# Softmax denominators turned by DMA instead of TensorE, and the values' bias folded into the output bias

## The chip, the cores and the metric

The kernel runs on one core of one Trainium2 chip. The metric is the device time of one execution in microseconds (us). The engines of the core are named as in the profile: PE (TensorE, matmuls), DVE (VectorE), ACT (ScalarE), POOL (GpSimd) and SP (SyncE, which here only issues DMAs). PE writes its products to PSUM, everything else lies in SBUF.

## The reference

The input is x, 16 batches of 512 tokens with 512 features. A layer norm is followed by an attention block and a gated FFN that run side by side on the normed x; both are added to x.

```python
xn = layernorm(x)
q, k, v = split(xn @ w_qkv.T + b_qkv)            # 16 heads of 32
attn = softmax(mask(q @ k.T / sqrt(32)))         # causal, 512 x 512 per head
a = (attn @ v) @ w_out.T + b_out
g, u = (xn @ gate_w.T) * gate_s, (xn @ up_w.T) * up_s   # 1408 wide, weights -1, 0, 1
f = ((silu(g) * u) @ down_w.T) * down_s
out = x + a + f
```

Everything is float32 in the reference.

## The kernel before

**Halves.** A float32 operand is held as two float16 tiles, a high half h and a low half l = x - h. A product of two such operands is three matmuls (h h, h l, l h). The FFN weights are exact in 8 bits and need one tile, so a product there is two matmuls. A "full" matmul contracts 128 rows and streams 512 columns. Making the halves is the work of the other engines: usually ACT casts the high half and POOL or DVE subtracts.

**Slots.** Work is cut into 64 slots, one for each batch b and group g of four heads. In slot s PE computes the scores of group s (`soft_run`, three runs of query blocks: block 3, block 2, blocks 1 and 0) and the value product of group s - 1 (`av_step`); in between it works on fillers: the q and k projections of the next group (`qk_proj`), the values of a batch (`v_proj`, in its first slot), FFN chunks (`ffn_chunk`), the down projection (`down_tile`, in the last slot of a batch) and the output projection of the batch before (`out_tile`).

**The softmax.** DVE adds the mask and takes the row maximum (L559), ACT takes the exponential and sums each row (L564) into `den`, 16 columns of 128 query rows: four query blocks by four heads. ACT and DVE split the exponentials into the halves `pq` (L584, L589), and SP issues a DMA transpose of each query block's `pq` into `pT` (L598). `pT` has single buffers, `pq` two.

**The denominators.** The value product comes out with (head, feature) on the 128 partitions and the 512 queries along the row, so it has to be multiplied by a tile that holds 1/den of the query, the same on the 32 partitions of a head. `av_step` makes it so: DVE takes the reciprocal `rden` (L618), POOL spreads each of its 16 columns over 32 (`rb`, L621), PE transposes the four 128x128 blocks of `rb` against an identity into the PSUM tile `R` (L631), and ACT copies `R` to SBUF as `Rs` (L634). After the value product `av` (72 matmuls of 32 columns of the array, four side by side, L644), DVE multiplies it with `Rs` (L657), ACT casts the high half `oh` (L658) and POOL subtracts to `ol` (L659). `out_tile` takes these.

**The values.** `v_proj` has 12 full matmuls for each of four token blocks. DVE scales the PSUM tile and adds the bias `bv_b`, which a DMA has spread to all partitions (L497), ACT casts `vh` (L500), POOL subtracts `vl` (L503).

**PSUM.** Projections, FFN tiles and `R` share three buffers with the tag "mm"; scores have four ("s1"), the value product one ("av").

**What sets the order.** The order on every engine is written out by a planner, `Plan`. Each step has an engine, a duration that the source assumes, what it reads and writes, and for PE a key: its wanted place in time. `Plan.order` simulates the five engines and the buffers with these durations; PE takes the lowest key among the steps that could start, the others the step that has been ready longest (plus a slack that the source gives). The resulting lists are fixed; at run time each engine goes through its list in order, and semaphores make it wait for what it reads. `attention_slot` gives the value product its key by `AV_LAG`, 7 us after the start of its slot, and the transposes of `R` 1.5 us before it. SP's list mixes the transposes of `pq`, those of the normed x of the next batch (`xh`, `xl`, L414), loads and stores.

**The bound checks.** A second, general path follows when a count of checked ranges is short of 48; on these inputs it isn't run.

Of the kernel before, what the change touches and what calls it, by code (L numbers as in the profile page):

```python
# [14 lines left out]
ALU = mybir.AluOpType  # L15
# [14 lines left out]
def newton_rsqrt(nc, y, v, t):  # L30

    yi = y.bitcast(I32)
    nc.vector.tensor_scalar(yi, v.bitcast(I32), 1, None, ALU.logical_shift_right)
    nc.vector.tensor_scalar(yi, yi, -1, 0x5F3759DF, ALU.mult, ALU.add)
    for _ in range(3):
        nc.vector.scalar_tensor_tensor(t, v, -0.5, y, ALU.mult, ALU.mult)
        nc.vector.tensor_tensor(t, t, y, ALU.mult)
        nc.vector.scalar_tensor_tensor(y, t, 1.5, y, ALU.add, ALU.mult)

# [23 lines left out]
class Plan:  # L63
# [34 lines left out]
    def order(self):  # L98
# [6 lines left out]
        made, done, dma = {}, [], 0.0  # L105

# [22 lines left out]
        while len(done) < len(self.steps):  # L129
            best = None  # L130
            for e in self.ENGINES:
                cands = [(max(t, free[e]), st) for t, st in ((begin(st), st) for st in ready[e]) if t is not None]
                if not cands:
                    continue
# [29 lines left out]
def fast_path(ctx, tc, good, x, wqkvT, bqk, bv, woT, bo, wgT, wuT, wdT, gs, us, dsc, out):  # L164
# [19 lines left out]
    def tmp32(name):  # L184
        return work(name, "tmp32", 4)
# [13 lines left out]
    bv_b = cp.tile([P, 512], F32, name="bv_b")  # L199
# [22 lines left out]
    grp = {}  # L222
# [20 lines left out]
    def mm_group(f, ps, ops, piece=4, first=0, n=None):  # L243
# [9 lines left out]
        prev = []  # L253
# [66 lines left out]
    def small_constants():  # L320
        gsus = work("gsus", "r32", 1)
        gs_c, us_c = (lambda: gsus()[:, 0:IC]), (lambda: gsus()[:, IC : 2 * IC])
        for dst, src, tok in ((bv_b, bv, "bv"), (ds_b, dsc, "ds"), (bo_b, bo, "bo")):
# [6 lines left out]
        add(  # L330
            "DVE", dve(512), lambda: nc.vector.tensor_scalar(bv_b, bv_b, 32.0, None, ALU.mult),
            r=["bv"], w=["bv"],
        )
        absmax(42, bqk_c[:, 0:4], ["bqk"])
        absmax(43, bqk_c[:, 4:8], ["bqk"])
        absmax(44, bv_b, ["bv"])
# [34 lines left out]
    def ln_stats(b, slack):  # L371
# [17 lines left out]
        add("DVE", 2.0, rstd, r=[(mv, tb) for tb in range(NT)], w=[v, y, t], slack=slack)  # L389
# [56 lines left out]
    def qk_proj(f, b, g, which):  # L446
# [15 lines left out]
            ],  # L462
        )
# [13 lines left out]
    def v_proj(f, b, tb):  # L477
        s = st[b]
        ps, t = mm(f"v_{b}_{tb}"), tmp32(f"vt_{b}_{tb}")
        if tb == 0:  # L480
# [12 lines left out]
            ],  # L493
        )
        add(
            "DVE", dve(512),
            lambda: nc.vector.scalar_tensor_tensor(t(), ps(), 2.0 ** -13, bv_b, ALU.mult, ALU.add),  # L497
            r=[ps, "bv"], w=[t], slack=-3,
        )
        add("ACT", act(512), lambda: nc.scalar.copy(vh()[:, tb, :], t()), r=[t], w=[(vh, tb)], slack=4)  # L500
        add(
            "POOL", gps(512),
            lambda: nc.gpsimd.tensor_tensor(vl()[:, tb, :], t(), vh()[:, tb, :], ALU.subtract),  # L503
            r=[t, (vh, tb)], w=[(vl, tb)], slack=2,
# [3 lines left out]
    def soft_run(b, g, blocks):  # L508
# [31 lines left out]
        def exps(i):  # L540
# [4 lines left out]
            "PE", 0.3 + 3 * cols / 2400.0, scores, r=[qh, ql, kh, kl],  # L545
# [31 lines left out]
        for i in blocks:  # L577
# [10 lines left out]
                "DVE", dve(4 * n),  # L588
# [12 lines left out]
            base += 8 * n  # L601
        return run

    def av_step(b, g):
# [6 lines left out]
        rb = work("rb_" + nm, "tmp32", 4)  # L611
        R = mm("R_" + nm)
        r = work("Rs_" + nm, "r32", 1)
# [4 lines left out]
        add("DVE", 0.15, lambda: nc.vector.reciprocal(rden(), d["den"]()), r=dens, w=[rden], slack=2)  # L618
        add(
            "POOL", gps(512),  # L620
            lambda: nc.gpsimd.tensor_scalar(  # L621
                rb().rearrange("p (c d) -> p c d", d=32),
                rden().unsqueeze(2).to_broadcast([P, 16, 32]),
                2.0 ** -15, None, ALU.mult,
            ),
            r=[rden], w=[rb],
        )

        def spread():
            for i in range(4):  # L630
                nc.tensor.transpose(R()[:, i * P : (i + 1) * P], rb()[:, i * P : (i + 1) * P], ident)  # L631

        first = add("PE", 0.5, spread, r=[rb], w=[R], lat=0.3)
        add("ACT", act(512), lambda: nc.scalar.copy(r(), R()), r=[R], w=[r], slack=-3)  # L634

        def run():
# [16 lines left out]
        second = add(  # L653
            "PE", 2.3, run, r=[("pT", i) for i in range(4)] + [(t, tb) for t in (vh, vl) for tb in range(NT)],
            w=[av], lat=0.3,
        )
        add("DVE", dve(512), lambda: nc.vector.tensor_tensor(r(), av(), r(), ALU.mult), r=[av, r], w=[r], slack=-2)  # L657
        add("ACT", act(512), lambda: nc.scalar.copy(oh(), r()), r=[r], w=[oh], slack=3)  # L658
        add("POOL", gps(512), lambda: nc.gpsimd.tensor_tensor(ol(), r(), oh(), ALU.subtract), r=[r, oh], w=[ol])  # L659
        return first, second  # L660
# [138 lines left out]
    def count_good(when, key):  # L799
        ps, ps1, limits = mm("flagT"), mm("flagR"), tmp32("limits")  # L800
# [8 lines left out]
        def set_limits():  # L809
# [9 lines left out]
            nc.gpsimd.memset(hi[:, 44:45], 64 * 32.0)  # L819
# [22 lines left out]
    def attention_slot(s):  # L842

        av, runs = (), []
# [7 lines left out]
        def place(t0, T):  # L852
            for k, step in enumerate(av):
                step.key = t0 + AV_LAG + (k - 1) * 1.5 if s < NSLOT else t0
            t = t0
            for step, c in runs:
                step.key = t
                t += T * c / sum(c for _, c in runs)

# [4 lines left out]
    AV_LAG = 7.0  # L864
    ends = []

    def fillers(s):
# [10 lines left out]
        if b > 0 and g in (1, 3):  # L878
            for tb in range(late) if g == 1 else range(late, NT):
                out_tile(f, b - 1, tb)  # L880
        for ic in range(CUTS[g], CUTS[g + 1]):
            ffn_chunk(f, b, ic)
        if g == 0 and b > 0:
# [42 lines left out]
    for s in range(NSLOT):  # L926
# [9 lines left out]
        if s == 2:  # L936
            for kc in range(KC):
                load_wo(kc)
        if g == 0 and b + 1 < NB:
            ln_load(b + 1, when)  # L940
            ln_stats(b + 1, 6.0)
            for tb in range(NT):
                ln_norm(b + 1, tb, 6.0)
                ln_turn(b + 1, tb, 6.0)
# [22 lines left out]
def general_path(ctx, tc, x, wqkvT, bqk, bv, woT, bo, wgT, wuT, wdT, gs, us, dsc, out):  # L967
# [21 lines left out]
    b_c = cp.tile([P, 8], F32, name="g_bqk")  # L989
    gs_c = cp.tile([P, IC], F32, name="g_gs")  # L990
    us_c = cp.tile([P, IC], F32, name="g_us")
    for dst, src in ((b_c, bqk), (gs_c, gs), (us_c, us)):
        nc.sync.dma_start(dst, src)
    bv_b = cp.tile([P, 512], F32, name="g_bv")
    bo_b = cp.tile([P, 512], F32, name="g_bo")
    ds_b = cp.tile([P, 512], F32, name="g_ds")
    for dst, src in ((bv_b, bv), (bo_b, bo), (ds_b, dsc)):
        nc.sync.dma_start(dst, src.partition_broadcast(P))

    with tc.For_i(0, NB, 1) as b:  # L1000
# [29 lines left out]
        for tb in range(NT):  # L1030
# [9 lines left out]
            nc.vector.tensor_tensor(v[:, tb, :], ps, bv_b, ALU.add)  # L1040
# [120 lines left out]
```

## Time and profile before

| | |
|---|---|
| median of 3 runs | 1909.89 us (1909.24 to 1911.51) |
| the profiled execution | 1909.74 us |
| its span, first to last instruction | 1908.0 us |
| mean granted PE clock | 0.997 |
| busy: PE, DVE, ACT, POOL | 98%, 78%, 70%, 52% of the span |
| DMA: hardware queues | 65.6% of 16 engines |

A line of the groups view names the line of the source, the engine, the operation, out<-in, the shapes and the count; then the busy time in us and the mean of one instruction in ns; then the idle time just before these instructions and what ended it. The waits view has, for each engine and line, what ended its idle time, the total in us, how often, and the longest. In a timeline the columns are start in us, length in us, engine, line, operation and count. A matmul's length holds the way through the array, which overlaps with the next one's: to see what a matmul costs, take the difference of two starts. A window's line has start and end, length, busy time and instruction count of PE, PE's weight loads, DVE, ACT and POOL, the granted clock, the DMA share and GB/s.

### The profile page before, as it was taken

How to read it: one execution, taken by the hardware profiler on the slowest of the kernel's cores; microseconds unless marked ns; L12 is line 12 of the kernel's file. 1: busy time of each engine (PE TensorE's matmuls, PEld its weight loads, DVE VectorE, ACT ScalarE, POOL GpSimd, SP SyncE). 2: the span in 40 equal slices, each digit the busy share in tenths (PEclk: the TensorE clock that was granted, in tenths of full speed). 3: DMA queues.
4: the chain of work that ended last, by engine and by line, in shares of the span. 5: the costliest groups of instructions: out<-in, count | busy, mean ns of one | idle time of the engine just before them, and what ended most of it. 6: DMA issues, size and time to landing. Idle time of an engine off the chain costs nothing. (4 is left out here: it accounts for less than half of the span.)

```text
span 1908.0 us, 40895 instructions
## 1 busy us (share of the span) xinstructions
PE 1877.7 (98%) x15250; PEld 893.3 (47%) x15250; DVE 1485.7 (78%) x3535; ACT 1334.9 (70%) x3179; POOL 986.7 (52%) x713
## 2 busy tenths in 40 slices
PE   7999999999999999999999999999999999999998
PEld 3444444444444444444444444444444444444444
DVE  8778678797887978868788687877869777686684
ACT  6766857677676777767767676785767767677773
POOL 4446455464554646456464454645546455463642
PEclk9999999999999999999999999999999999999999
DMA  9866667666686656767567676676866768666654
GB/s 177 146 130 117 124 135 154 132 123 124 132 155 122 149 108 138 143 135 145 112 131 146 122 148 121 135 127 138 155 129 128 119 137 149 127 133 103 127 110 103
DMA packets 770447, 252.39 MB, mean 132 GB/s; under 512 B 734272, under 2 KB 740800, under 8 KB 770240
## 3 DMA queue, kind: packets, MB, share of 16 engines
q1 hardware_dynamic: 765616, 247.54, 65.6%
q0 software_dynamic: 4624, 2.16, 1.4%
q8 instruction: 121, 1.98, 0.4%
q14 instruction: 86, 0.70, 0.1%
HBM read 55.85 MB, written 16.78 MB: 38 GB/s over the span
## 5 line engine op out<-in xcount | busy, mean ns | idle before, releaser
L564 ACT ACTIVATE p<-s,negm 128x512 f32<-128x512 f32 (+3 forms) x1024 | 530.0, 532 | 224.9 <-DVE negm L559 222.7
L589 DVE SCALAR_TENSOR_TENSOR pq<-p,pq 128x2048 f16<-128x2048 f32 (+3 forms) x256 | 428.0, 1686 | 232.9 <-ACT pq L584 228.5
L559 DVE CUSTOM_DVE_ANT_0 s<-s,mask 128x512 f32<-128x512 f32 (+3 forms) x1024 | 472.9, 517 | 46.4 <-PE s L530 37.6
L584 ACT ACTIVATE pq<-p 128x2048 f16<-128x2048 f32 (+3 forms) x256 | 324.1, 1291 | 12.1 <-DMA pT<-pq 10.3
L694 POOL TENSOR_TENSOR hl<-ft,hh 128x512 f16<-128x512 f32 x176 | 227.6, 1299 | 193.1 <-ACT hh L693 192.4
L472 POOL TENSOR_TENSOR qkl<-qkt,qkh 128x512 f16<-128x512 f32 x128 | 167.1, 1306 | 238.6 <-ACT qkh L470 231.9
L251 PE MATMUL g<-xh,wg 128*128 128x512 f16 x704 | 268.4, 381 | 5.0 <-ACT qkt L467 3.3
L251 PE MATMUL u<-xh,wu 128*128 128x512 f16 x704 | 267.4, 380 | 4.5 <-ACT qkt L467 2.7
L251 PE MATMUL dn<-wd,hh 128*128 128x512 fp8e4 x704 | 268.3, 381 | 0.0
L251 PE MATMUL g<-xl,wg 128*128 128x512 f16 x704 | 267.8, 380 | 0.0
L251 PE MATMUL dn<-wd,hl 128*128 128x512 fp8e4 x704 | 267.6, 380 | 0.0
L251 PE MATMUL u<-xl,wu 128*128 128x512 f16 x704 | 267.6, 380 | 0.0
L693 ACT CAST hh<-ft 128x512 f16<-128x512 f32 x176 | 109.5, 623 | 174.5 <-DVE ft L690 174.4
L621 POOL TENSOR_SCALAR rb<-rden 128x512 f32<-128x512 f32 x64 | 136.4, 2132 | 165.4 <-DVE rden L618 165.4
L251 PEld LDWEIGHTS <-wu 128*128 128x128 fp8e4 x1408 | 137.5, 98 | 171.6 <-issue 8.1
L564 ACT ACTIVATION_READ_ACCUMULATOR p<-s,negm 128x1 f32 x1024 | 214.8, 210 | 0.0
L251 PEld LDWEIGHTS <-wg 128*128 128x128 fp8e4 x1408 | 132.9, 98 | 160.9 <-issue 12.3
L251 PEld LDWEIGHTS <-wq_h 128*128 128x128 f16 x1024 | 95.1, 98 | 132.9 <-issue 26.7
L680 ACT ACTIVATE ft<-g,gt_c 128x512 f32<-128x512 f32 x176 | 121.4, 690 | 42.2 <-PE g L251 40.5
L410 POOL TENSOR_TENSOR xnl<-xc,xnh 128x512 f16<-128x512 f32 x60 | 96.5, 1609 | 102.7 <-DMA xl<-xnl 60.0
L659 POOL TENSOR_TENSOR ol<-Rs,oh 128x512 f16<-128x512 f32 x64 | 98.8, 1544 | 96.7 <-ACT oh L658 96.6
L690 DVE SCALAR_TENSOR_TENSOR ft<-u,gu_c,ft 128x512 f32<-128x512 f32 x176 | 132.0, 750 | 21.0 <-PE u L251 4.9
(114 smaller groups left out, 3202.6 us busy)
## 6 DMA issues: line engine op xcount, KB each, us to landing
xc<-in_x SPq DMA_DIRECT2D x64, 256.0 KB, 3.9
xr<-in_x SPq DMA_DIRECT2D x64, 256.0 KB, 3.0
out<-y SPq DMA_DIRECT2D x64, 256.0 KB, 2.5
pT<-pq SPq DMA_TRANSPOSE x256, 5.5
exact<-in_wdT SPq DMA_DIRECT2D x11, 256.0 KB, 2.9
exact<-in_wgT SPq DMA_DIRECT2D x8, 256.0 KB, 2.9
exact<-in_wuT SPq DMA_DIRECT2D x8, 256.0 KB, 2.9
wq<-in_wqkvT SPq DMA_DIRECT2D x2, 768.0 KB, 6.6
```

What stands on the lines that cost most here:

```text
L251: nc.tensor.matmul(ps(), l, r, start=(first + k == 0), stop=(first + k == n - 1))
L472: "POOL", gps(512), lambda: nc.gpsimd.tensor_tensor(l(), t(), h(), ALU.subtract),
L559: nc.vector.tensor_tensor_reduce(sc, sc, mask[:, 512 - n :], -(2.0 ** -7), 3e38, ALU.add, ALU.min, negm()[:, m : m + 1])
L564: nc.scalar.activation(exps(i).rearrange("p (k j) q -> p k j q", j=4)[:, :, j, :], part().rearrange("p (k q) -> p k q", q=P), AF.Exp, bias ...
L584: "ACT", act(4 * n), lambda src=src, half=half: nc.scalar.mul(half(0), src(), 2.0 ** 15),
L589: lambda src=src, half=half: nc.vector.scalar_tensor_tensor(half(1), src(), 2.0 ** 15, half(0), ALU.mult, ALU.subtract),
L621: lambda: nc.gpsimd.tensor_scalar(rb().rearrange("p (c d) -> p c d", d=32), rden().unsqueeze(2).to_broadcast([P, 16, 32]), 2.0 ** -15, Non ...
L659: add("POOL", gps(512), lambda: nc.gpsimd.tensor_tensor(ol(), r(), oh(), ALU.subtract), r=[r, oh], w=[ol])
L680: "ACT", act(512) + 0.1, lambda: nc.scalar.activation(t(), pg(), AF.Tanh, scale=gt_c[:, ic : ic + 1]),
L690: lambda: nc.vector.scalar_tensor_tensor(t(), pu(), gu_c[:, ic : ic + 1], t(), ALU.mult, ALU.mult),
L693: add("ACT", act(512), lambda: nc.scalar.copy(hh(), t()), r=[t], w=[hh], slack=3)
L694: add("POOL", gps(512), lambda: nc.gpsimd.tensor_tensor(hl(), t(), hh(), ALU.subtract), r=[t, hh], w=[hl])
```

## The change

**Denominators.** DVE takes the reciprocal and splits it into two float16 halves `rh` (128x16 each, scaled by 2^12). ACT spreads both over 32 columns each into `rb`, now 128x1024 in float16. SP issues one DMA transpose of its eight 128x128 blocks into the SBUF tile `R`. POOL adds the high and the low blocks to `Rs`, and DVE's multiply takes the scale back. PE has no part in it, and `R` is no longer in PSUM.

**Values.** `v_proj` adds no bias. ACT casts `vh` straight from PSUM, then DVE makes `vl` from PSUM and `vh`; POOL has no part. Since the rows of a softmax sum to one, the bias passes through the value product unchanged, so bv @ w_out.T can be added to the output bias once: `bias_proj`, in slot 2, makes halves of bv spread over 128 columns, 12 full matmuls and one DVE operation on `bo_b`. The bias is loaded as 128x4.

**The planner.** PE may take only steps whose key lies within 20 of the lowest key that is not yet done (`AHEAD`). Some assumed durations change. The value product is placed by key directly behind the second score run of its slot. Steps of `qk_proj` and `v_proj` get an extra order behind earlier score runs and value products. The later `out_tile` calls move from the last slot of a batch to the end of the third; layer-norm steps get more slack; the tag "tmp32" has five buffers instead of four.

```diff
+AHEAD = 20.0
...
+                if e == "PE":
+
+                    cands = [c for c in cands if c[1].key <= keys[-1][0] + AHEAD]
...
+            after=last_scores[b * NG + g - 2 : b * NG + g - 1] if b * NG + g > 1 else (),
...
+            after=[grp[(b - 1, NG - 1)]["step"]] if b else (),
+        )
+
+        add("ACT", act(512), lambda: nc.scalar.mul(vh()[:, tb, :], ps(), 2.0 ** -13), r=[ps], w=[(vh, tb)], slack=-3)
         add(
             "DVE", dve(512),
-            lambda: nc.vector.scalar_tensor_tensor(t(), ps(), 2.0 ** -13, bv_b, ALU.mult, ALU.add),
-            r=[ps, "bv"], w=[t], slack=-3,
-        )
-        add("ACT", act(512), lambda: nc.scalar.copy(vh()[:, tb, :], t()), r=[t], w=[(vh, tb)], slack=4)
-        add(
-            "POOL", gps(512),
-            lambda: nc.gpsimd.tensor_tensor(vl()[:, tb, :], t(), vh()[:, tb, :], ALU.subtract),
-            r=[t, (vh, tb)], w=[(vl, tb)], slack=2,
+            lambda: nc.vector.scalar_tensor_tensor(
+                vl()[:, tb, :], ps(), 2.0 ** -13, vh()[:, tb, :], ALU.mult, ALU.subtract
+            ),
+            r=[ps, (vh, tb)], w=[(vl, tb)], slack=-3,
         )
+
+    def bias_proj(f):
+
+        ps = mm("bvo")
+        hl = work("bvhl", "y", 4, (P, 2, KC, P), F16)
+        h, l = (lambda: hl()[:, 0]), (lambda: hl()[:, 1])
+        wide = bv_c.unsqueeze(2).to_broadcast([P, KC, P])
...
+        mm_group(
+            f, ps,
+            [
+                ((lambda kc=kc, u=u, w=w: (u()[:, kc, :], w[:, kc, :])), [hl, (wt, kc)])
+                for kc in range(KC)
+                for u, wt, w in ((h, "woh", wo_h), (h, "wol", wo_l), (l, "woh", wo_h))
+            ],
+        )
+        add(
+            "DVE", dve(512),
+            lambda: nc.vector.scalar_tensor_tensor(bo_b, ps(), 2.0 ** -16, bo_b, ALU.mult, ALU.add),
+            r=[ps, "bo"], w=["bo"], slack=-3,
+        )
...
-        add("DVE", 0.15, lambda: nc.vector.reciprocal(rden(), d["den"]()), r=dens, w=[rden], slack=2)
+
+        def halves():
+            nc.vector.reciprocal(rden(), d["den"]())
+            nc.vector.tensor_scalar(rh()[:, 0, :], rden(), 2.0 ** 12, None, ALU.mult)
+            nc.vector.scalar_tensor_tensor(rh()[:, 1, :], rden(), 2.0 ** 12, rh()[:, 0, :], ALU.mult, ALU.subtract)
+
+
+        add("DVE", 0.6, halves, r=dens, w=[rden, rh], slack=2)
+        add(
+            "ACT", act(1024),
+            lambda: nc.scalar.copy(
+                rb().rearrange("p (c d) -> p c d", d=32),
+                rh().rearrange("p z c -> p (z c)").unsqueeze(2).to_broadcast([P, 32, 32]),
+            ),
+            r=[rh], w=[rb], slack=4,
+        )
+        add("SP", 1.3, lambda: nc.sync.dma_start_transpose(R(), rb()), r=[rb], w=[R], lat=1.5)
         add(
             "POOL", gps(512),
-            lambda: nc.gpsimd.tensor_scalar(
-                rb().rearrange("p (c d) -> p c d", d=32),
-                rden().unsqueeze(2).to_broadcast([P, 16, 32]),
-                2.0 ** -15, None, ALU.mult,
+            lambda: nc.gpsimd.tensor_tensor(
+                r(), R()[:, 0:4, :].rearrange("p i q -> p (i q)"), R()[:, 4:8, :].rearrange("p i q -> p (i q)"), ALU.add
             ),
-            r=[rden], w=[rb],
-        )
-
-        def spread():
-            for i in range(4):
-                nc.tensor.transpose(R()[:, i * P : (i + 1) * P], rb()[:, i * P : (i + 1) * P], ident)
-
-        first = add("PE", 0.5, spread, r=[rb], w=[R], lat=0.3)
-        add("ACT", act(512), lambda: nc.scalar.copy(r(), R()), r=[R], w=[r], slack=-3)
+            r=[R], w=[r],
+        )
...
-            for k, step in enumerate(av):
-                step.key = t0 + AV_LAG + (k - 1) * 1.5 if s < NSLOT else t0
             t = t0
-            for step, c in runs:
+            for k, (step, c) in enumerate(runs):
+                if k == 1 and av:
+                    av.key = t + 0.01
                 step.key = t
                 t += T * c / sum(c for _, c in runs)
+            if not runs:
+                av.key = t0
...
-        if b > 0 and g in (1, 3):
-            for tb in range(late) if g == 1 else range(late, NT):
+        if b > 0 and g == 1:
+            for tb in range(late):
                 out_tile(f, b - 1, tb)
         for ic in range(CUTS[g], CUTS[g + 1]):
             ffn_chunk(f, b, ic)
+        if b > 0 and g == 2:
+            for tb in range(late, NT):
+                out_tile(f, b - 1, tb)
```

## The prediction

> **What bounds the kernel now.** I read the share of busy time first, then the windows, then who waited for whom on PE.
>
> ```profile
> span 1908.0 us, 40895 instructions
> ...
> PE 1877.7 (98%) x15250; PEld 893.3 (47%) x15250; DVE 1485.7 (78%) x3535; ACT 1334.9 (70%) x3179; POOL 986.7 (52%) x713
> ```
>
> A pipelined PE always looks busy, so 98% alone proves little. The first fence below is a window of the steady part (start and end, length, then busy time of each engine with instruction counts); the second has PE's waits over the whole run (total us, times, longest).
>
> ```profile
> 250.00:1800.00 1550.00, 1550.00 (x12643) 738.19 (x12642) 1221.34 (x2927) 1099.32 (x2640) 823.07 (x575) 1.00 0.67 133
> ```
> ```profile
> PE lnT L426 <- DVE xc L396: 10.1, 1, 10.1
> PE g L251 <- ACT qkt L467: 3.3, 1, 3.3
> PE R L631 <- POOL rb L621: 2.9, 1, 2.9
> PE u L251 <- ACT qkt L467: 2.7, 2, 1.7
> ```
>
> Between 250 and 1800 us PE is never idle, and asking that window for PE's waits gives no row. All waits lie in the first 210 us and around 1834 us. So in the steady part the time is the sum of what PE issues: an instruction taken off PE shortens the run by its issue interval, as long as no other engine becomes late. The other engines have room (DVE 79% of that window, ACT 71%, POOL 53%, DMA 67%).
>
> **The PE transposes that go.** The timeline of one slot (start, length, engine, line):
>
> ```profile
> 700.50 1.03 PE L251 MATMUL qk<-xh,wq_l 128*128 128x512 f16 x4
> 701.36 0.60 PE L631 MATMUL R<-ident,rb 128*128 128x128 f32 x4
> 701.80 0.38 PE L251 MATMUL dn<-wd,hh 128*128 128x512 fp8e4 x1
> 702.01 0.38 PE L251 MATMUL dn<-wd,hl 128*128 128x512 fp8e4 x1
> ```
>
> Lengths overlap; starts count. Full matmuls start 0.216 us apart (0.86 for four); the four transposes hold PE from 701.36 to 701.80, 0.436 us (4 x 0.109). 64 slots: **-27.9 us**. The one wait of a transpose, 2.9 us at 110 us, goes too, with the half-clock stretch it set off (seven matmuls started about 0.43 instead of 0.216 us apart, 1.5 us): **-4.4**.
>
> The transposes also held one of the three "mm" PSUM buffers. The 3.3 us wait of g at 55 us is for a buffer that ACT empties late, and about 1.6 us of half clock follows it. Without R, g takes the buffer before it, and the late one is needed only by u, eight matmuls (1.7 us) later. Between 0 and the whole 4.9 us; I take **-2**, the 1.7 and a little of the clock.
>
> **What is added to PE.** The bias product: 12 full matmuls once, 12 x 0.216 = **+2.6**. Passing between full-array matmuls and the 32-wide score or value products costs 0.09 to 0.10 us each time (702.45 to 702.75 above such a step instead of 0.216). In the order of the changed program there are 492 such passages instead of 480: 12 x 0.095 = **+1.1**. The value product does not come directly behind the second score run in most slots, since its pT is not in at that point of the plan.
>
> **What moves to other engines, per slot.** DVE gains two 128x16 operations; nearest are the 128x4 ones at 0.16 us and the reciprocal at 0.24: 0.33 us. ACT loses the R copy and gains a 128x1024 spread; POOL loses the broadcast multiply and gains an addition of 128x512:
>
> ```profile
> L634 ACT COPY Rs<-R 128x512 f32<-128x512 f32 x64 | 38.9, 607 | 4.6 <-PE R L631 4.6
> L584 ACT ACTIVATE pq<-p 128x1024 f16<-128x1024 f32 x64 | 69.3, 1083 | 10.4 <-DMA pT<-pq 10.3
> L621 POOL TENSOR_SCALAR rb<-rden 128x512 f32<-128x512 f32 x64 | 136.4, 2132 | 165.4 <-DVE rden L618 165.4
> L503 POOL TENSOR_TENSOR vl<-vt,vh 128x512 f16<-128x512 f32 x64 | 80.1, 1262 | 9.1 <-ACT vh L500 9.0
> ```
>
> (out<-in, count | busy us, mean ns | idle before.) ACT +1.08 - 0.61 = +0.48 us; POOL -2.13 + 1.26. The values, per tile: one DVE operation of 0.68 stays one, one ACT cast stays one (now from PSUM, first), and POOL loses the 1.26 of vl. Per batch DVE goes from 91.8 us in 116.5 to 93.1 in about 114.8, 81%; ACT from 82.6 to 84.6, 74%. Neither becomes the bound on the mean: 0. A value tile in PSUM is now held for ACT and then DVE (0.63 + 0.68 with their queues) where DVE alone emptied it; three buffers and 2.6 us per tile of 12 matmuls hide this, and if they did not, 16 batches at up to 1 us give 16.
>
> **The new DMA transpose** is the disputed step: SP issues in order, R waits there for ACT's spread, and the value product waits for the last pT transpose. Around the tightest slot:
>
> ```profile
> 1222.05 2.00 SPq L598 DMA_TRANSPOSE pT<-pq  x1
> 1224.14 1.59 SPq L414 DMA_TRANSPOSE xh<-xnh  x1
> 1226.18 1.23 SPq L598 DMA_TRANSPOSE pT<-pq  x1
> ```
> ```profile
> 1230.48 0.29 PE L644 MATMUL av<-pT,vh 128*32 128x256 f16 x4
> ```
>
> The last pT (eight 128x128 blocks, as many as R has) takes 1.23 us to issue and lands 3.1 us after its start, at 1229.3; the product starts 1.2 us later. For the four groups of a steady batch this cover is about 1.2, 2.3, 3.1 and 4.3 us (landings and starts of the trace). In the changed order R of the first group stands between the same two pT transposes, in the place of that xh: 1.3 us for 1.2 to 1.6, nothing gained or lost. R of groups two and three is new ahead of the last pT (1.3 us later), R of the fourth follows it. PE's work from the last scores to the product, its instructions in both orders counted at the intervals above, grows from 19.2, 20.1, 16.9, 16.1 to 19.8, 25.0, 20.6, 19.7 us, so the covers, R's 1.3 left out, become about 1.8, 7.2, 6.8, 7.9. R's own chain is 0.56 (DVE), 1.1 (ACT), 1.3 (SP) within 3.1 to landing, 1.3 (POOL): 6 us and its queues, against 12.5 to 14 us between reciprocal and DVE's multiply in the trace. DMA's transposes grow from 88 to 96 blocks a slot, its share from 0.67 to about 0.72. I take 0.
>
> Here a rule of the Trainium skill speaks against the change: "VectorE: DVE Perf Modes", The three transpose paths, prices a 128x128 bf16 transpose at 390 ns on TensorE and 1309 ns by DMA, and its rules for authors say TensorE if PSUM will do. Eight blocks at 1.309 would be an estimated 10.5 us, 7.4 more than the trace's 3.1. Then the pT behind R would be 7.4 late: 5.6 + 0.2 + 0.6 = 6.4 us of PE stall a batch, 102 in all, and the run would take about 1985. The row shows eight blocks in 3.1 us, so the row decides.
>
> **The tail.** Before, the last value product (1890.80 to 1892.6) is followed by 27 output matmuls of the first three groups (5.8 us), which hide DVE, ACT and POOL making oh and ol:
>
> ```profile
> 1892.75 0.69 DVE L657 TENSOR_TENSOR Rs<-av,Rs 128x512 f32<-128x512 f32 x1 [3.09 <-PE av L644]
> 1893.47 0.62 ACT L658 CAST oh<-Rs 128x512 f16<-128x512 f32 x1 [8.62 <-DVE Rs L657]
> ```
>
> In the changed order all 36 of those matmuls stand ahead of the product, and the twelve that need oh and ol directly behind it. PE then waits about 1.5 us for oh (1892.6 to 1894.1), starts two, waits about 0.8 for POOL's ol: +2.5 with the steps between. This trace has the half clock after idles of 3.3 and 2.9 us, and once, at 1837, after one of only 1.7. "TensorE: Matmul & The Clock Gate", The HAM clock gate, has it after an idle window of about 3.4 us, which would spare these two waits and leave +2.5; with the third row in mind the twelve matmuls may run at half clock, 2.6 more. I take the middle: **+3.8**.
>
> **Sum.** -27.9 - 4.4 - 2 + 2.6 + 1.1 + 3.8 = -26.8; 1908.0 - 26.8 = 1881.2 of span. The profiled execution took 1909.74, 1.74 more than its span, and the median is 0.15 above that: **1883 us**, 1.4% less. The early waits (about 17 us with their half clocks) and those near 1834 (3.6) come out of a new order and can go either way by some 6 us.
>
> **Rivals.**
> (a) The order also empties the early and the 1834 us waits: 10 us less, 1873. For: POOL is relieved by 2.1 us a slot, 14% of its busy time, and the 256 KB broadcast of bv goes. Against: most of those waits are ACT's, behind DMA that is 90% busy there.
> (b) R makes the last pT late: SP waits at R for ACT's spread, which stands behind ACT's last pq copy. If that costs the first group 2.8 us against its 1.8, 16 stalls of 1.0 give 16: 1899. For: that cover is the thinnest. Against: both ACT pieces precede the DVE half of pq, which the last pT waits for anyway.
> (c) Nothing to see: PE's 0.44 us a slot is only traded for waits on DVE, 1908 to 1912. Against: 21% of DVE's time is idle and PE never waits in 1550 us.
> (d) Slower: R lands after DVE wants to multiply. DVE is in order, so score maxima, the FFN halves and PSUM's buffers wait behind it, then PE. It decides from 26.8/64 = 0.42 us of PE stall a slot. If R came 8 us later than I add up, 14 against 13, with 1 us of stall a slot: 64 - 27 = +37, 1947. Against: 6 us against 12.5.
> The change could also fail to remove R from PE; the order has no transposes left there, so no.
>
> **Numbers.** Forecast 0.68, (a) 0.12, (b) 0.12, (c) 0.03, (d) 0.05. Range 1870 to 1899, from below (a) to (b), leaves out (c), (d) and the edges of (a) and (b). A measurement tells 0.2%, 3.8 us, from no change. Faster: forecast, (a), (b) and a fifth of (c): 0.93; same 0.02; slower 0.05.
>
> **What would show it.** 256 - 12 = 244 fewer PE matmuls, no R rows, no PE waits in a window like 300 to 1750, a batch of 114.8 us instead of 116.5 (value product to value product). Last group: two PE waits below 2 us. Wrong if value products wait on a DMA (b), if DVE's multiply has idle time before it put down to POOL (d), or if half-clock stretches grow.

## The result and the profile after

The changed kernel takes **1895.56 us** (median of 6 runs, 1894.85 to 1898.61), the kernel before 1909.57 beside it: a ratio of 0.993 (95% interval 0.9917 to 0.9943). It is faster by 14.0 us, about half of the 26.8 forecast; 1895.56 lies inside the range 1870 to 1899, towards its slow end. The profiled execution took 1895.28 us, its span is 1893.5.

The page's first rows, with the 244 fewer matmuls that the prediction counts (15250 before):

```profile
span 1893.5 us, 40528 instructions
...
PE 1856.3 (98%) x15006; PEld 863.7 (46%) x15006; DVE 1526.5 (81%) x3665; ACT 1377.2 (73%) x3179; POOL 846.2 (45%) x649
```

The same window as before (start and end, length, busy time of PE, PEld, DVE, ACT, POOL, clock, DMA share):

```profile
250.00:1800.00 1550.00, 1546.10 (x12607) 720.31 (x12606) 1264.09 (x3058) 1147.92 (x2663) 703.80 (x527) 1.00 0.74 143
```

PE, never idle there before, is now idle for 3.9 us. Who it waits for over the whole run (total us, times, longest):

```profile
PE lnT L432 <- DVE xc L402: 10.7, 1, 10.7
...
PE u L260 <- DVE ft L727: 6.4, 8, 1.6
PE s L562 <- ACT p L596: 3.1, 5, 1.3
PE u L260 <- ACT qkt L474: 2.9, 1, 2.9
PE s L562 <- ACT qkh L477: 2.9, 1, 2.9
PE v L260 <- DVE ft L727: 1.8, 1, 1.8
PE op L260 <- ACT oh L700: 1.5, 1, 1.5
...
PE op L260 <- POOLq L1175: 0.6, 1, 0.6
```

The wait of R for POOL is gone, and so is that of g for qkt, but other waits of the early part stand in their place (u for qkt, s for p and qkh, v for ft). No value product waits for pT, and neither PE nor DVE waits for R (POOL's addition does, 3.3 us in all 64 slots). Six of the eight waits of u for DVE's ft lie between 250 and 1780 us, where before none did.

The new work costs about what was forecast (count, then busy us, mean ns, idle before): the spread 1.06 us (1.08 forecast), the two half operations 0.21 and 0.18 (0.33 together), POOL's addition 1.19 (1.26); vh and vl are one operation each, straight from PSUM.

```profile
L663 ACT COPY rb<-rh 128x1024 f16<-128x1024 f16 x64 | 68.0, 1063 | 4.0 <-DVE rh L657 3.5
L656 DVE TENSOR_SCALAR rh<-rden 128x16 f16<-128x16 f32 x64 | 13.2, 206 | 2.2
L657 DVE SCALAR_TENSOR_TENSOR rh<-rden,rh 128x16 f16<-128x16 f32 x64 | 11.2, 175 | 2.2
L672 POOL TENSOR_TENSOR Rs<-R 128x512 f32<-128x512 f16 x64 | 75.8, 1185 | 3.3 <-DMA R<-rb 3.3
L504 ACT ACTIVATE vh<-v 128x512 f16<-128x512 f32 x64 | 38.5, 602 | 15.8 <-PE v L260 15.7
L507 DVE SCALAR_TENSOR_TENSOR vl<-v,vh 128x512 f16<-128x512 f32 x64 | 43.6, 681 | 4.8 <-ACT vh L504 4.8
```

**Where the time went.** I compared where each slot's first score matmul starts in the two traces. "Slot 12 to slot 62" is the steady part below: 50 slots.

| part | before, us | after, us | difference | the forecast's share |
|---|---|---|---|---|
| start to slot 12 | 374.6 | 374.4 | -0.2 | -8.7: eleven to twelve slots of 0.436, -4.4, -2, +2.6, a few switches |
| slot 12 to slot 62 | 1453.2 | 1438.4 | -14.8 | -20.8: 50 x 0.436 less 1.0 of switches |
| slot 62 to the end of the span | 80.2 | 80.7 | +0.5 | +2.7, what is left of -26.8: +3.8, less two slots and their switches |

So 6 us are missing in the steady part and 8.5 in the early one; the end is 2 us better than forecast. From value product to value product a steady batch takes 116.5 us before; after, it takes 114.9 in five of eleven, next to the 114.8 forecast, and 115.9 in five others (117.6 in the last).

### The profile page after: what moved, and what is told of

It reads as the page before. It is cut to its first block, busy times and chain, and to the rows that moved or that the text cites. A ratio compares the mean times of both kernels' runs of the same rounds, so it can differ in the third digit from the quotient of the medians.

```text
span 1893.5 us, 40528 instructions
## 1 busy us (share of the span) xinstructions
PE 1856.3 (98%) x15006; PEld 863.7 (46%) x15006; DVE 1526.5 (81%) x3665; ACT 1377.2 (73%) x3179; POOL 846.2 (45%) x649
## 5 line engine op out<-in xcount | busy, mean ns | idle before, releaser
L621 DVE SCALAR_TENSOR_TENSOR pq<-p,pq 128x2048 f16<-128x2048 f32 (+3 forms) x256 | 413.8, 1623 | 150.1 <-ACT pq L616 149.2
L737 POOL TENSOR_TENSOR hl<-ft,hh 128x512 f16<-128x512 f32 x176 | 246.1, 1400 | 372.8 <-ACT hh L736 372.6
L479 POOL TENSOR_TENSOR qkl<-qkt,qkh 128x512 f16<-128x512 f32 x128 | 160.0, 1250 | 248.0 <-ACT qkh L477 247.6
L701 POOL TENSOR_TENSOR ol<-Rs,oh 128x512 f16<-128x512 f32 x64 | 103.3, 1613 | 203.0 <-ACT oh L700 202.8
L727 DVE SCALAR_TENSOR_TENSOR ft<-ft,g 128x512 f32<-128x512 f32 x176 | 119.8, 680 | 51.7 <-ACT ft L723 51.0
L767 POOL TENSOR_TENSOR xr<-xr,bo_b 128x512 f32<-128x512 f32 x64 | 84.4, 1321 | 163.0 <-DMA xr<-in_x 152.3
```

Of the source, the lines that this page charges most:

```text
L479: "POOL", gps(512), lambda: nc.gpsimd.tensor_tensor(l(), t(), h(), ALU.subtract),
L621: lambda src=src, half=half: nc.vector.scalar_tensor_tensor(half(1), src(), 2.0 ** 15, half(0), ALU.mult, ALU.subtract),
L727: "DVE", dve(512), lambda: nc.vector.scalar_tensor_tensor(t(), t(), 1.0, pg(), ALU.add, ALU.mult),
L737: add("POOL", gps(512), lambda: nc.gpsimd.tensor_tensor(hl(), t(), hh(), ALU.subtract), r=[t, hh], w=[hl])
```

## Experiments

Each time is a median; ratios are to the kernel before on the same chip, with their 95% interval. The last column is slot 12 to slot 62 against the kernel before, from the profiles.

| kernel | us | ratio | steady part, us |
|---|---|---|---|
| before | 1907.8 to 1909.6 | 1 | 0 |
| before, R's transposes off | 1908.42 | 0.9996 (0.9988 to 1.0004) | +1.1 |
| before, new order, transposes kept | 1930.49 | 1.0112 (1.0096 to 1.0127) | +18.0 |
| before, new order, transposes off | 1895.23 | 0.993 (0.9917 to 0.9944) | -9.3 |
| changed | 1895.56 | 0.993 (0.9917 to 0.9943) | -14.8 |
| changed, once more | 1896.18 | 0.9937 (0.9923 to 0.995) | -14.9 |
| changed, four transposes back on PE | 1919.45 | 1.0059 (1.0045 to 1.0073) | +7.0 |
| changed, R by DMA twice | 1897.20 | 0.9935 (0.9921 to 0.9948) | -20.7 |
| changed, exact check's DVE work out | 1891.76 | 0.9907 (0.9893 to 0.9921) | -20.1 |
| changed, LN's slack 6 | 1889.61 | 0.9903 (0.9889 to 0.9917) | -19.5 |
| the same, once more | 1891.17 | 0.9905 (0.989 to 0.992) | -19.0 |

### Is an instruction off PE worth its interval?

This is the assumption under the largest term. The first experiment takes R's transposes off the kernel before and leaves every order as it is (but for one pair of DVE operations that are swapped at 208 us):

```
-            for i in range(4):
-                nc.tensor.transpose(R()[:, i * P : (i + 1) * P], rb()[:, i * P : (i + 1) * P], ident)
+            pass
-        add("ACT", act(512), lambda: nc.scalar.copy(r(), R()), r=[R], w=[r], slack=-3)
+        add("ACT", act(512), lambda: nc.scalar.copy(r(), rb()), r=[R, rb], w=[r], slack=-3)
```

> The kernel before with the transposes of the spread reciprocals left out on PE and ACT copying the untransposed tile in their place (the output is scaled by the wrong query's denominator); all orders are the same. My prediction's terms: -27.9 for the matmuls and -4.4 for the wait and half clock at 110 us, -2 for the freed PSUM buffer, so 1875.5. Rival (the early waits belong to late DVE and ACT work, and pass to the next PE instruction): the matmuls alone, 1880 to 1883, with about as much early waiting as before.

It measured 1908.42 us. Both expectations failed: 27.9 us taken off an engine that never waited were worth 1 us. PE's waits between 250 and 1780 us, where the kernel before has none:

```profile
PE av L643 <- DMA pT<-pq: 7.5, 5, 1.7
PE u L251 <- DVE ft L683: 4.1, 9, 0.6
PE v L251 <- DVE ft L683: 3.6, 13, 0.3
```

These 15.2 us are only the waits that the profile names. Measured from matmul to matmul between slots 12 and 62, everything was given back: value products start 10.4 us later than at the old intervals, u 6.6, v 5.2 and output matmuls 0.7, together 22.9 us for the 21.8 that the transposes took there. PE ran 0.44 us a slot faster until it met pT and DVE's ft, which had been arriving just in time.

The second experiment gives the same kernel, without transposes, the order rules of the changed one and plans it anew:

```
-                step.key = t0 + AV_LAG + (k - 1) * 1.5 if s < NSLOT else t0
+                if k == 1 and av:
+                    av[1].key = t + 0.01
...
-        if b > 0 and g in (1, 3):
-            for tb in range(late) if g == 1 else range(late, NT):
+        if b > 0 and g == 1:
+            for tb in range(late):
...
+        if b > 0 and g == 2:
+            for tb in range(late, NT):
+                out_tile(f, b - 1, tb)
...
-            ln_stats(b + 1, 6.0)
+            ln_stats(b + 1, 12.0)
```

> The kernel before without R's transposes (as in the experiment that took them off; R is again a copy of the unspread tile, so the output is not the reference's), values and bias as before, and with the order of the changed kernel planned for it: value product placed behind the second score run, output tiles in the second and third slot of a batch, LN's slack 12, PE at most 20 us ahead in the plan. PE's work from last scores to value product becomes 18.8, 25.0, 20.6, 19.7 us for the four groups (15.6 to 19.7 without the new order). If it is the new order that lets PE's saving through, 1884 to 1894. If the value halves straight from PSUM (two engines instead of three, POOL relieved) are what is needed, the waits on DVE and ACT stay and it is 1902 to 1909. In the first case the waits of value products for pT (7.5 us in 250 to 1780) must be gone except in the first group of a batch, whose distance is unchanged.

It measured 1895.23 us, just past the first case's 1894, without the DMA transposes of R and without values straight from PSUM. It is level with the changed kernel only in total: its steady part is 5.5 us longer, its early part 5.4 us shorter. The waits for pT are gone, in the first group of a batch too, where the expectation would have let them stay; DVE's remain (250 to 1780 us):

```profile
PE u L260 <- DVE ft L693: 8.3, 12, 0.7
PE u L260 <- DVE y L755: 2.2, 4, 0.6
```

The third keeps the transposes and takes only the order; the diff is the one above, with the transposes placed ahead of the value product.

> The kernel before with all its work, R's transposes on PE too, in the order of the changed kernel (the order rules of the experiment before it, R's transposes placed ahead of the value product; PE's work from last scores to value product 19.2, 24.5, 20.1, 20.1 us). The order alone. If PE sets the pace in both orders as long as it carries the transposes, the order alone cannot shorten the steady part: from slot 12 to slot 62 no more than 2 us either way against before, in all 1904 to 1911 (early part up to 5 us shorter, tail about 2.5 to 4 longer). If the new order is by itself what is worth the time and the transposes never mattered, 1895 to 1899, as without the transposes in this order (1895.2).

1930.49 us: slower than any kernel here, and neither of the two cases. In the steady part it is 18.0 us longer than the kernel before, and 15.5 us of named waits appear:

```profile
PE u L260 <- DVE y L760: 7.4, 9, 1.1
PE u L260 <- DVE ft L698: 6.2, 9, 0.7
PE s L541 <- ACT p L575: 1.9, 5, 0.4
```

So taking the transposes off is worth 1 us in the old order and 35 in the new one. Not all of the 35 is the price of the transposes: in the steady part it is 27.3 us, against the 21.8 that they take there. The planner moves other steps too when a PE step is absent, so the last two orders differ in details (PE's work from last scores to value product of the second group is 24.5 us in one and 25.0 in the other), and R also holds one of the three "mm" buffers in the third kernel; these two are not told apart. Neither taking the transposes off nor the order brings anything by itself.

The fourth puts four transposes of a constant tile back on PE in the changed kernel, ahead of each value product, with all other orders kept:

```
         def run():
+            for i in range(4):
+                nc.tensor.transpose(av()[:, i * P : (i + 1) * P], ident, ident)
```

> The changed kernel with four transposes of a constant 128x128 fp32 tile put back on PE directly ahead of each value product (they write the product's own PSUM tile, which the product then overwrites; the output is the same). It prices PE's 0.436 us a slot in the changed order. If the changed order leaves the other engines room, so that PE alone sets the pace there, it costs 27.9 us less what it absorbs of the waits in the steady part (4 to 6 us): 1917 to 1924, slower than before. If other engines set the pace in the changed kernel as they seem to in the one before without transposes (where taking the transposes off gave 1 us), most of it disappears in their waits: 1896 to 1904.

> The changed kernel once more, unchanged, as the yardstick beside the next three: 1895.6 us within 1.5 either way by every theory. Its profile should again show the only PE waits of 250 to 1780 us as u waiting for DVE's ft, 3 to 5 us in total; early waits may differ by 1 to 3 us between profiles of the same program, as they seemed to in the experiment on the tail.

1919.45 against 1896.18 us: +23.3, as the first case has it. In the steady part it is 7.0 + 14.9 = 21.9 us, 0.438 a slot: the interval that the prediction read from the trace. (That it fits so closely is in part chance: u's named waits for ft fell from 3.8 to 2.6 us, and in the 17 slots where scores come directly before the product, the transposes add one more passage of 0.1 us between full-array and 32-wide matmuls.) In the changed order PE does set the pace.

The kernels differ in what the prediction calls cover, the time from the last pT's landing to the start of the value product. Mean us for the four groups of a batch, slots 12 to 59:

| kernel | group 1 | 2 | 3 | 4 |
|---|---|---|---|---|
| before | 0.9 | 2.2 | 2.7 | 4.0 |
| before, transposes off | -1.1 | 1.5 | 2.1 | 3.8 |
| before, new order, transposes off | 3.5 | 3.2 | 3.4 | 6.8 |
| before, new order, transposes kept | 3.8 | 2.8 | 3.0 | 8.1 |
| changed | 3.2 | 4.2 | 3.1 | 6.5 |
| changed, R by DMA twice | 0.4 | 1.6 | 0.8 | 5.6 |

A negative mean: the landing that the trace gives is later than the start of the product that waited for it. Group 1 gains 4.6 us between the second and third line although PE's work between its last scores and its product is 18.8 us in both. It comes from the other engines' order: DVE ends the last half of `pq` 16.4 us after group 1's last score matmul in the second line and 11.1 in the third (means), while from there to the landing takes 3.9 and 4.2 us, so the queue is not where it is gained. In the order of the kernel before, DVE normalises the next batch (xc) in the first slot of a batch, 36 of 48 times in the second line's trace; in the new order all 48 lie in the second. That this is the step that made DVE late is likely, not shown: I didn't take the order's rules apart one by one. Cover is not the whole account either. With the transposes kept, the new order has as much of it as the fast kernels; its named waits are for DVE's y and ft and ACT's p instead.

### What does the DMA transpose of R cost?

```
+        def turn():
+            for _ in range(2):
+                nc.sync.dma_start_transpose(R(), rb())
```

> The changed kernel with every transpose of R issued twice in a row into the same tile (same result), all orders else as they are: it prices the new DMA step by one more of it. By the trace of the changed kernel one more R holds SP 1.23 us, the last pT of groups one to three lands that much later against covers of 2.6 to 4.8 us before the value product, and POOL's addition starts 1.3 to 2 us later against 4 to 9 us up to DVE's multiply: hidden in the steady part, 0 to 2 us in all with the early slots, 1896 to 1898. If the DMA queue is what binds and R was paid for with a late pT, each of the 64 costs about 0.5 to 1.2 us of PE: 1928 to 1970, with PE's waits of value products for pT in the steady part.

1897.20 us, 1.0 above the changed kernel, and no wait at all of PE between 250 and 1780 us. The cover table shows the price: 2.3 to 2.8 us of cover for groups 1 to 3, and it just fitted (0.4 and 0.8 us left). So one R is hidden in the steady part, two are as well, and by these covers a third would not be (an estimate; it wasn't run). Only the early part pays, 6.9 us up to slot 12, most of it in one wait for pT:

```profile
PE av L690 <- DMA pT<-pq: 4.9, 2, 4.4
```

An R of 1.78 us and the pT behind it in a first group of the changed kernel, POOL's addition and the value product (start, length):

```profile
750.63 1.78 SPq L669 DMA_TRANSPOSE R<-rb  x1
752.50 1.28 SPq L630 DMA_TRANSPOSE pT<-pq  x1
...
755.78 1.15 POOL L672 TENSOR_TENSOR Rs<-R 128x512 f32<-128x512 f16 x1
...
759.24 0.29 PE L686 MATMUL av<-pT,vh 128*32 128x256 f16 x4
```

That pT landed at 756.6, 4.1 us after its start and 2.6 ahead of the product; eight blocks at the 1309 ns that the prediction weighed would have been 10.5.

The surprise is that the steady part got 5.9 us *shorter* than the changed kernel's: -20.7, next to the -20.8 of the forecast. That leads to the next question.

### Where are the missing 6 us of the steady part?

My theory was that DVE runs over in the second slot of a batch, where LN's slack of 12 put LN's work beside the exact check's, y and scores, so that ft is late for u (0.80 and 0.17 us, in six of the eleven batches). DVE is busy for 96% of that slot in the changed kernel, 89% in the kernel before (means of slots 12 to 59). Two experiments take DVE work out of that slot: the exact check's two operations are left out in all its 35 pieces (its flags are set to zero instead), or LN's slack goes back to 6.

```
-            lambda: nc.vector.tensor_reduce(
-                ranges[:, 16 + k : 17 + k], t()[:, :n], AX.X, ALU.max, apply_absolute_value=True
-            ),
+            lambda: None,
...
```

> The changed kernel without the two DVE operations of each check that the FFN weights are exact (35 times 1.45 us; their loads stay, the flags are set to zero), so this part of the range check is left out; every engine's order is otherwise the same. Theory (in the second slot of a batch DVE has more work than time, and u waits for it): the waits of u on ft, six pairs of 0.8 and 0.17 us, vanish, 5 to 7 us less, about 1889.5. Rival (these waits come from ACT or from the new R chain): they stay and the time stays within 2 us of the changed kernel.

```
-            ln_stats(b + 1, 12.0)
+            ln_stats(b + 1, 6.0)
-                ln_norm(b + 1, tb, 12.0)
-                ln_turn(b + 1, tb, 8.0)
+                ln_norm(b + 1, tb, 6.0)
+                ln_turn(b + 1, tb, 6.0)
```

> The changed kernel with the layer-norm steps' slack back at 6, so that DVE makes the statistics and the inverse deviation for the next batch in the first slot of a batch, the normalisation still in the second. Theory (the slack moved DVE work into the second slot, where it overflows): most of the waits of u on ft in the steady part go, 3 to 6 us less. Rival (the small operations of R and the later outputs fill the slot in any case): within 2 us of the changed kernel, the waits still there.

> The changed kernel with LN's slack back at 6, once more beside the two others: 1889.6 within 1.5 either way if the gain of 6 us over the changed kernel (1895.6 and 1896.2 in two measurements) is the steady part's, which does not vary between profiles.

They measured 1891.76, 1889.61 and 1891.17 us, with steady parts of -20.1, -19.5 and -19.0. The first gained 3.8 us on the changed kernel where 5 to 7 were expected. In its profile the steady part is 5.3 us shorter, with no PE wait between 250 and 1780 us, and the early part 2.6 us longer. The second kernel has this one wait there, and two of 0.5 us when it was measured once more:

```profile
PE u L260 <- DVE ft L727: 0.5, 1, 0.5
```

The theory holds for the steady part, and LN's slack of 6 in the changed kernel makes the fastest kernel of this study. But the second R took no work off DVE, and its waits went as well. DVE's own rows answer that. LN's groups between 250 and 1780 us in the kernel before:

```profile
L396 DVE TENSOR_SCALAR xc<-xc,mv,ln_y 128x512 f32<-128x512 f32 x52 | 25.8, 539 | 0.0
L36 DVE SCALAR_TENSOR_TENSOR ln_t<-ln_v,ln_y 128x4 f32<-128x4 f32 x39 | 6.3, 162 | 1.3
L37 DVE TENSOR_TENSOR ln_t<-ln_t,ln_y 128x4 f32<-128x4 f32 x39 | 6.3, 162 | 1.3
```

In the changed kernel:

```profile
L402 DVE TENSOR_SCALAR xc<-xc,mv,ln_y 128x512 f32<-128x512 f32 x52 | 43.8, 889 | 0.3
L36 DVE SCALAR_TENSOR_TENSOR ln_t<-ln_v,ln_y 128x4 f32<-128x4 f32 x39 | 17.0, 436 | 1.3
L37 DVE TENSOR_TENSOR ln_t<-ln_t,ln_y 128x4 f32<-128x4 f32 x39 | 14.6, 375 | 1.3
```

The same operations take 1.6 to 2.7 times as long. One by one: a 128x4 operation that overlaps no POOL operation takes 0.16 us in every case; one that begins while POOL runs an elementwise operation takes up to 1.15, and mostly ends about 20 ns after that operation. A 128x512 xc takes 0.54, or up to 1.5 with POOL on qkl, xnl or Rs. In the kernel before none of them met POOL. The two engines' timelines in the second slot of a batch:

```profile
757.18 3.77 DVE L402 TENSOR_SCALAR xc<-xc,mv,ln_y 128x512 f32<-128x512 f32 x4
...
757.19 1.16 POOL L479 TENSOR_TENSOR qkl<-qkt,qkh 128x512 f16<-128x512 f32 x1 [0.26 <-ACT qkh L477]
759.51 1.17 POOL L416 TENSOR_TENSOR xnl<-xc,xnh 128x512 f16<-128x512 f32 x1 [1.16 <-ACT xnh L415]
```

Four xc take 3.77 us where they would take 2.2. Added up over a batch and set beside u's late starts in it: in the two profiles of the changed kernel, 22 steady batches, all twelve in which LN was stretched by 3.7 us lost 0.97 us on PE; the other ten, stretched by 2.7 or less, lost nothing. With the second R, POOL's addition came later, past LN's first operations; the stretch was 0.8 to 1.8 us a batch, and no u was late. With the exact check out, eight of eleven batches had 3.4 to 3.7, and u lost 0.2 or nothing, as DVE had less else to do. That POOL's timing decides between 0 and 1 us of PE a batch fits all of these; no run moved POOL alone.

### Can the tail and the early part be mended?

In the tail the value product follows all 36 output matmuls of the first three groups. The experiment puts 27 of them behind it:

```
+    for steps in partial[1:]:
+        steps[0].deps.add(grp[(NB - 1, NG - 1)]["step"])
```

> The changed kernel with one order edit at the very end: the output matmuls of token blocks 1 to 3 over the first three groups (27 of them) stand behind the last value product again, as in the kernel before. Theory (the tail's two PE waits of 1.6 and 0.8 us and the half clock after them are owed to that order): 3.5 to 4.5 us less than the changed kernel, about 1891.5, and no PE wait between the last value product and the last matmul. Rival (the wait only moves, since pT or R land late at the end): less than 1 us gained.

1899.65 us, ratio 0.9952 (0.9939 to 0.9964), 4.1 more than the changed kernel. The rival held: the wait moved from oh to pT, and from slot 63 to PE's last instruction took 1.9 us more.

```profile
PE av L686 <- DMA pT<-pq: 4.4, 1, 4.4
```

The profiled execution was the slowest of the five (1901.96), 6.7 us above the changed kernel's. Of these, 3.3 were lost by slot 5, where every engine has the same order as in the changed kernel: early parts of one order can differ by so much.

For the early part I suspected the weight loads, issued by POOL, that share the DMA engines with the first slot's pT transposes, and moved seven of these nine loads behind the first hl:

```
-    done = plan.order()
+    done = [st for st in plan.order() if st not in late_loads]
+    k = done.index(slot_runs[1])
+    done[k + 1 : k + 1] = late_loads
```

> The changed kernel with LN's slack back at 6 (1889.6 when it was measured alone) and, with every order on PE, DVE and ACT kept, the last two of three pieces of wg and wu and all of wd issued on POOL behind the first hl product instead of ahead of it. Theory: the early waits come from these loads sharing the DMA engines with the pT transposes of the first slot (4.9 us each there, 3.1 later), so ACT waits 7.3 us for a pq buffer and PE 2.9 us for qkt at 56 us, followed by about 3 us of half clock. Then 1883 to 1887. If the loads are not the cause, or only wait later for u and g of the second slot, 1888 to 1891.

1897.10 us, ratio 0.994 (0.9927 to 0.9954), worse than LN's slack alone. Second, with LN's slack alone PE waits 3.4 us at the bias product for the output weights, and I moved that product one slot later:

```
+        if s == 3:
             f = Fill()
             bias_proj(f)
```

> The changed kernel with LN's slack back at 6 and the bias product moved from the third to the fourth slot, so that PE doesn't wait 3.4 us there for the low half of the output weights. Steady part and tail as with LN's slack alone (slot 12 to slot 62: 19 to 20 us shorter than before). If the 3.4 us really are PE's and go, 1885 to 1888; if PE then waits elsewhere in the first five slots, as after the loads were moved, 1889 to 1893.

1910.38 us, ratio 1.0007 (0.9999 to 1.0015): its steady part is unchanged, and by slot 5 it is 19 us behind. The two largest of PE's waits in this last one, over the whole run:

```profile
PE g L260 <- ACT qkt L474: 11.5, 1, 11.5
PE s L562 <- ACT p L596: 11.5, 15, 3.0
```

With the loads moved, g waits 13.2 us for the same qkt. Both of my ideas failed. In neither was a wait of the first five slots a sum that could be taken away: another, longer one came up behind it.

## Why the prediction was right or wrong

The total came out inside the range, but at about half of the forecast's gain, and the slow end of the range stood at 1899 for the sake of rival (b), which did not come. That the range holds 1895.56 is luck; of the steady part's 20.8 us, 14.8 came.

- **The transposes, -27.9.** The interval of 0.436 us is right, measured back as 0.438 a slot in the changed order. The step that failed is the sentence that carries it, "in the steady part the time is the sum of what PE issues". From 1550 us without a wait I concluded that the other engines had room. The window shows only that nothing was late at that pace; taking the transposes off in the same order was worth 1 us. I had a number that should have warned me, the first group's 1.2 us of cover, and used it for R alone. That the change still gained is due to its new order, in which the same transposes are worth their interval; that cover is 3.2 us there.
- **"Neither becomes the bound on the mean: 0".** DVE did not, on the mean (82% of the window), but it did in the second slot of a batch. This cost the missing 6 us: -14.8 instead of -20.8 in the steady part, and -19.0 to -20.7 in the four profiles where DVE's slot was relieved. I had priced DVE's operations from the old trace, and LN's do not keep their length beside POOL.
- **R by DMA, 0.** Right in the steady part, and with little margin: covers of 3.2, 4.2, 3.1, 6.5 against the 1.8, 5.9, 5.5, 7.9 that I worked out with R's 1.3 on groups two and three; a second R left 0.4. The row decided rightly over the 1309 ns that the Trainium skill gives ("VectorE: DVE Perf Modes", The three transpose paths).
- **Early waits, -6.4.** Wrong in whole. Both waits went, and others came in their place, so that slot 12 begins 0.2 us earlier instead of 8.7. I had put 6 us on either side of these waits and should have left them out of the sum. What sets the early part stays open: from -5.6 to +19.9 us among the kernels here.
- **The tail, +3.8.** Right for the last group: 1.5 and 0.6 us of named waits and seven matmuls 0.43 us apart behind them, 1.5 more (the lines below are the first). That the end as a whole is 2 us better than forecast is owed to other things: near 1836 us the kernel before waits 1.7 us for qkt and then runs at a granted clock of 0.50 (1836.9 to 1838.6 us, and part of what follows), where the changed one waits 1.6 us near 1833 and keeps a clock of 1.00; and the work behind the last matmul is 0.8 us shorter.

```profile
1882.24 0.39 PE L260 MATMUL op<-wo_h,oh 128*128 128x512 f16 x1 [1.52 <-ACT oh L700]
1882.47 0.38 PE L260 MATMUL op<-wo_l,oh 128*128 128x512 f16 x1
1883.47 0.52 PE L260 MATMUL op<-wo_h,ol 128*128 128x512 f16 x1 [0.63 <-POOLq L1175]
1883.78 0.63 PE L260 MATMUL op<-wo_h,oh 128*128 128x512 f16 x1
1884.21 0.63 PE L260 MATMUL op<-wo_l,oh 128*128 128x512 f16 x1
```

- **Rivals.** (a), (b) and (d) did not come: no early gain, no late pT, nothing waiting for R. (c), time on PE traded for waits on DVE, got 0.03 and is what holds for the kernel before without its transposes; in the changed kernel 5.8 of the steady part's 20.8 us went that way. My argument against it, "21% of DVE's time is idle and PE never waits", is refuted by that experiment.

## What to carry to other kernels

An engine that never waits may still be only one of several that finish together; before pricing an instruction taken off it, measure the covers of what it consumes, and where one is small, expect to gain little in that order. Removing work and reordering can be worth nothing apart and much together, so test each alone and both together. When a step is moved, look at what will then run beside it on the other engines, since its length may change.

## What the runs showed of the hardware

- Small DVE operations were stretched by POOL's elementwise operations: 0.16 to 1.15 us for 128x4, 0.54 to 1.5 for 128x512, both float32 in SBUF; where they outlast POOL's, the small ones end about 20 ns after it, the large ones mostly 0.28 us. The Trainium skill ("GPSIMD Engine Reference", Key points) says that POOL shares its SBUF interfaces with VectorE, with contention for VectorE instructions that have two SBUF inputs or run in a 2-port mode. The traces agree for the small operations, which have two SBUF inputs and last as long as the rest of POOL's; the large ones have one, and no run shows in which mode they go.
- PE ran at a granted clock of 0.50 (0.427 us from matmul to matmul instead of 0.216) for seven matmuls after two idles of only 1.5 and 0.6 us, with two matmuls between them. One idle of 1.65 us in the kernel before (1836 us) was followed by a clock of 0.50, one of 1.63 us in the changed kernel (1833 us) by 1.00.
